# A planned attention-and-feed-forward kernel: the 42 leftover features on quarters of the array, the last block by tiles, sums shared with GpSimd, and a new plan

## The chip, the cores and the metric

The kernel runs on one core of one Trainium2 chip. The metric is the device time of one execution in microseconds (us). The core has TensorE (PE in the profile, with PEld for its weight loads), VectorE (DVE), ScalarE (ACT), GpSimd (POOL) and SyncE (SP), which here only issues transfers (DMA). Each engine works through its own instructions strictly in the order in which they were written, and waits on semaphores for the others.

## The reference, cut to what matters

The input `x` has 4 sequences of 1024 tokens with 256 features, all in 32-bit floats. After a layer norm, two branches start from the same `xn`, and both are added to `x`:

```
xn  = layernorm(x)
out = x + attention(xn) + ffn_stack(xn)

attention: rms norm, q,k,v = xn @ W_qkv (16 heads of 64), softmax over a window of 64 keys
           back, times sigmoid(xn @ W_gates + b_gates) per head, @ W_out
ffn_stack, twice (DEPTH = 2):
    h = shift_token(x)                    # second half of the features comes from the token before
    q, k, v = split(h @ wqkv)             # 8 heads of 64
    q, k = l2norm and scale, then rotary:  q*cos*s + rotate_half(q)*sin*s
    o = attention over a window of 128 keys back
    x = x + o @ wo
    h = layernorm(shift_token(x))
    a, g = split(h @ w1 + b1)             # 682 features each
    x = x + (a * gelu(g)) @ w2 + b2       # 682 = 5*128 + 42
```

The 682 hidden features are five full groups of 128 and a tail of 42 (`TAIL`).

## The kernel before, in words

The tokens are cut into 16 blocks of 256 (`TB`), each of two tiles of 128 (`NT` = 2), four blocks to a sequence. There are 16 blocks of the first attention (`first_attention(n)`), then 16 of the first feed-forward layer (`layer(0, n)`) and 16 of the second (`layer(1, n)`); the first three blocks of layer 0 (`MIX` = 3) are begun between the last blocks of the first attention. A layer's block has an attention half and, behind a `yield`, a feed-forward half. `LAG` says how many blocks' attention halves are begun before the oldest feed-forward half is recorded. What a stage leaves for the next one is stored in DRAM buffers (`carried`) and fetched again.

Nothing is written to an engine directly. Every step is recorded by `op(...)` with its cost in us on each engine that could do it, its buffers and its dependencies; `Plan.run` then goes through all steps with a model of the five engines, picks the engine where there is a choice, the time and the buffer, and `emit` writes the instructions in that order. A step is due when the steps that use it need it. The plan's constants are `SLACK` (a factor on the costs of an engine), `LAT`, `LAND` (the landing of a transfer), `LOOK` (how far ahead of the oldest open step it may reach, in us of TensorE work), the spare buffers of each kind, and the price of turning TensorE between the whole array ("full") and quarters of it ("rc", `TURN` 3.0). A transfer of n columns costs n/465 us on SP in this plan. The order that comes out is fixed; on the chip an engine that comes late makes the others wait.

The steps that the change and the prediction speak of, by their lines in the profile:

- L973 projects q, k, v of a tile ("qkvb"); L1112 are the scores ("sb") and L1202 the weighted sum over values ("ob"), both as 64x64 matmuls on quarters of the array; L1227 is the projection with `wo` ("pw").
- L1041 (GpSimd) multiplies the rotated halves with sin, L1057 (VectorE) the row with cos, L1065 (VectorE) adds the two, L1083 scales k ("kn", on either engine).
- The feed-forward half: L1235 adds the residual ("y2"), L1249, L1252 and L1257 shift half of the features by one token through transfers, L1293 to L1300 are the statistics, L1309 and the power of L401 the deviation on GpSimd, L1321 (ScalarE) or L1323 (VectorE) the normalised rows, L462 and L471 send them through DRAM and back so that L479 (VectorE) can finish a transpose, and L1336 applies gain and offset ("d"). In the last block of all, `LATE`, TensorE transposes instead (L425, L450).
- L1362 is the projection up ("up"): for each of the five full groups 2 halves x 2 chunks of 256 columns, and for the tail one matmul a chunk whose weights hold both halves of the tail side by side. L1375 (ScalarE) is the gelu, L1382 (VectorE) adds the offset and multiplies.
- L1398 is the projection down ("down"): for each tile six matmuls in a row, one for each of five groups and one for the tail, where the unused rows of the operand are zero (L1346 clears them). L1409 adds the rest, L1418 stores the output.

In 32-bit floats the profile shows every matmul as two instructions: L1398 has 64 tiles x 6 matmuls = 384, and 768 instructions.

Of the kernel before, what the change touches and what calls it, by code (L numbers as in the profile page):

```python
# [44 lines left out]
N_D = 12  # L45
LAND = 4.0
LAG = 3
MIX = 3
BOTH = True

EARLY = {0, 1}
LATE = {(1, 15)}
FROM = 8, 11

# [21 lines left out]
class Plan:  # L76
    LAT = {"PE": 0.25, "DVE": 0.3, "ACT": 0.3, "POOL": 0.3, "SP": 2.0}
    SLACK = {"DVE": 1.15, "POOL": 1.15, "ACT": 1.1}
    SWITCH = {"PE": 0.1, "ACT": 1.4}
    TURN = {"PE": 3.0, "ACT": 40.0}  # L80
    IDLE = 300.0
    LOOK = 200.0
    DEAR = {"DVE": 3.0}
# [142 lines left out]
def layers_kernel(  # L226
# [41 lines left out]
        },  # L268
        {"w": (3, 0.05, 20), "g": (1, 0.0, 1), "s": (4, 0.05, 12), "ps": (0, 0.02, 3), "d": (1, 0.0, 1)},
    )  # L270
# [15 lines left out]
    def load_x(n):  # L286
        b, g = blocks[n]
        xs[n] = xb = buf("w")
        op(
            {"SP": 1.1},  # L290
            lambda e: nc.sync.dma_start(
                v2(xb, NT, DIM), x[b, g * TB : (g + 1) * TB].rearrange("(i p) f -> p i f", p=P)
            ),
            w=(xb,), name="x",
        )
# [20 lines left out]
    def unit(pieces, us=2.3):  # L316

        u = buf("w")
        for n, (to, m, of) in enumerate(pieces):

            def bring(e, to=to, m=m, of=of):
                nc.sync.dma_start(u.t[:, to : to + m], of)

            op({"SP": max(m / 465, 0.45)}, bring, a=(u,), lat=us, name="weights")
        return u
# [50 lines left out]
    def store(dst, src):  # L376
        op(
            {"SP": 1.1},
            lambda e: nc.sync.dma_start(rows_apart(dst.t, NT * DIM), v2(src, 4, NT * DIM // 4)),
            r=(src,), w=(dst,), lat=3.5, name="store",  # L380
        )

    def fetch(src, b):
        op(
            {"SP": 1.1},
            lambda e: nc.sync.dma_start(v2(b, 4, NT * DIM // 4), rows_apart(src.t, NT * DIM)),
            r=(src,), w=(b,), name="fetch",
        )
# [40 lines left out]
    def across(s, m, turned, near=False):  # L429

        n, f = 4 * 32 * m, 32 * m
        if near:
            bank = buf("ps")
            transposes(
                lambda: [
                    (bank.t[:, k * P : (k + 1) * P], s.t[:, k * P : (k + 1) * P]) for k in range(m)  # L440
                ],
                bank, (s,), "near", 0.109 * m,
            )
            for b, to, at, k in turned:

                def put(e, b=b, to=to, at=at, k=k):
                    at = slice(at * P, (at + k) * P)
                    of = bank.t[:, at].rearrange("p (k c j) -> p j k c", k=k, j=4)
                    if e == "ACT":
                        nc.scalar.copy(to(b), of)  # L450
                    else:
                        nc.vector.tensor_copy(to(b), of)

                op(
                    {"ACT": COPY[k * P][0], "DVE": COPY[k * P][1]}, put, r=(bank,), a=(b,),
                    name="near",
                )
            return
        d = buf("d")
        op(  # L460
            {"SP": n / 465},
            lambda e: nc.sync.dma_start(rows_apart(d.t, n), v2(s, 4, f)),  # L462
            r=(s,), w=(d,), lat=LAND, name="turn out",
        )
        turn_in(d, m, turned)

    def turn_in(d, m, turned):
        n, t = 4 * 32 * m, buf("w")
        op(
            {"SP": n / 465},  # L470
            lambda e: nc.sync.dma_start(  # L471
# [16 lines left out]
    def load_layer(l):  # L488
# [31 lines left out]
        for k, (n, c) in enumerate((n, c) for n in range(2) for c in range(NC)):  # L520
# [17 lines left out]
        )  # L538
        op(
            {"SP": 0.45},  # L540
            lambda e, u=u: nc.sync.dma_start(u.t[:TAIL, DIM : 2 * DIM], w2[l, full:, :]), w=(u,),
            name="weights",
        )
        w["b1"] = bb = const.tile([P, 2, NM], F32, name=f"b1{l}")
# [21 lines left out]
    def load_rotation(l):  # L566

        for k, src in ((0, cos_d), (1, sin_d)):
# [13 lines left out]
            for q in range(2):  # L582
                u = turn[k, q] = buf("w")
                op(
                    {"SP": 1.1},
                    lambda e, u=u, q=q, src=src: nc.sync.dma_start(
# [345 lines left out]
    def layer(l, n, before):  # L932
# [29 lines left out]
        before["y"] = y  # L962
        y2 = buf("w")
        for i in range(NT):
# [67 lines left out]
            for m in range(2):  # L1032
# [20 lines left out]
                def times_cos(e, rc=rc, m=m, raw=raw, ti=ti, cos=cos):  # L1053

                    f = v3(cos, 4, 2, D)[:, ti % 4, m].rearrange("p (a r) -> p a r", a=2)
                    for h in range(2):
# [6 lines left out]
                op(  # L1063
                    {"DVE": 0.61},
                    lambda e, rc=rc, rot=rot: nc.vector.tensor_tensor(  # L1065
                        rc.t[:, :512], rc.t[:, :512], rot.t[:, :512], ALU.add
# [158 lines left out]
            def project_out(e, pw=pw, oT=oT):  # L1225
                for p in range(PB):
# [8 lines left out]
                lambda e, pw=pw, i=i: nc.vector.tensor_tensor(  # L1235
                    v3(y2, 2, NT, P)[:, :, i, :].rearrange("p c (a r) -> p c a r", a=4),
                    v3(pw, NC, 4, 32), by_feature(xb, i), ALU.add,
                ),
                r=(pw, xb), a=(y2,), name="y2",
            )  # L1240

        yield

        sh = buf("w")
        S = lambda: v2(sh, NT, P)
        y2_old = before.get("y2")

        def shift(e):
            nc.sync.dma_start(S()[0:1, 1, :], v3(y2, 2, NT, P)[P - 1 :, 1, 0, :])  # L1249

            for lo, hi in ((0, P - 16), (P - 16, P - 1)):
                nc.sync.dma_start(S()[lo + 1 : hi + 1], v3(y2, 2, NT, P)[lo:hi, 1])  # L1252

        if g:
            op(
                {"SP": 0.5},
                lambda e: nc.sync.dma_start(  # L1257
                    S()[0:1, 0, :], v3(y2_old, 2, NT, P)[P - 1 :, 1, NT - 1, :]
                ),
# [4 lines left out]
        op({"SP": 1.2}, shift, r=(y2,), a=(sh,), lat=2.4, name="sh")  # L1264
        before["y2"] = y2

# [5 lines left out]
        else:  # L1272
# [7 lines left out]
            lambda e: nc.gpsimd.tensor_tensor(  # L1280
                v3(rest, NT, 2, P), v3(y2, 2, NT, P).rearrange("p h i f -> p i h f"), to(), ALU.add
            ),
# [7 lines left out]
        def stats(e, h):  # L1290
            for i in range(NT):
                of = v3(y2, 2, NT, P)[:, 0, i, :] if h == 0 else S()[:, i, :]
                nc.vector.bn_stats(st_at(i, h), of)  # L1293
            if h:
                for i in range(NT):
                    nc.vector.bn_aggr(
                        st.t[:, 24 + 2 * i : 26 + 2 * i], st.t[:, 12 * i : 12 * i + 12]
                    )
                var = st.t[:, 24:28].rearrange("p (i s) -> p i s", i=NT)[:, :, 1]
                nc.vector.tensor_scalar_add(st.t[:, 28:30], var, EPS)  # L1300

# [4 lines left out]
        def deviation(e):  # L1306
            rsqrt(st.t[:, 30:32], st.t[:, 28:30])
            for i in range(NT):
                nc.gpsimd.tensor_scalar(shift_by(i), mean(i), rstd(i), -1.0, ALU.mult, ALU.mult)  # L1309
# [3 lines left out]
        for h in range(2):  # L1313

            def normal(e, h=h):
                for i in range(NT):
                    of = v3(y2, 2, NT, P)[:, 0, i, :] if h == 0 else S()[:, i, :]
# [10 lines left out]
        d = buf("w")  # L1328
        across(nn, 4, [(d, lambda b: b.t[:, :512].rearrange("p (k c j) -> p j k c", k=4, j=4), 0, 4)], (l, n) in LATE)

        def affine(e):
            for c in range(NC):
                at = slice(c * TB, (c + 1) * TB)
                g_, b_ = w["v"][:, 0, c : c + 1], w["v"][:, 1, c : c + 1]
# [13 lines left out]
        for m in range(NM):  # L1348
# [5 lines left out]
            def up(e, pf=pf, m=m, tail=tail):  # L1354
                for n_ in (0,) if tail else (1, 0):
                    for c in range(NC):
                        if tail:
                            wt = w["w1e"].t[:, c * P : (c + 1) * P]
                        else:
                            u, at, step = w["w1"][n_, m]  # L1360
                            wt = u.t[:, c * step + at : c * step + at + P]
                        nc.tensor.matmul(  # L1362
                            pf.t[:, n_ * TB : (n_ + 1) * TB], wt, d.t[:, c * TB : (c + 1) * TB],
                            start=(c == 0), stop=(c == NC - 1),
                        )

            op(
                {"PE": 0.86 if tail else 1.72}, up, r=(d, *us), w=(pf,),
                mode="full", name="up",
            )  # L1370

            def gelu(e, pf=pf, ge=ge, m=m, tail=tail, k=k):
                u = P // 2 if tail else 0
                at = slice(0, TB) if tail else slice(TB, 2 * TB)
                nc.scalar.activation(  # L1375
                    ge.t[:k], pf.t[u : u + k, at], AF.Gelu, bias=w["b1"][u : u + k, 1, m : m + 1]
                )

            op({"ACT": 0.39}, gelu, r=(pf, w["b_vec"]), w=(ge,), mode="gelu", name="gelu")

            def gated(e, pf=pf, ge=ge, m=m, k=k):
                nc.vector.scalar_tensor_tensor(  # L1382
                    gT[m // 2].t[:k, (m % 2) * TB : (m % 2 + 1) * TB], pf.t[:k, :TB],
                    w["b1"][:k, 0, m : m + 1], ge.t[:k], ALU.add, ALU.mult,
                )
# [5 lines left out]
        xo, xos = buf("w"), [buf("w") for _ in range(NT)]  # L1391
        for i in range(NT):
            pz = buf("ps")

            def down(e, pz=pz, i=i):
                for m in range(NM):
                    at = (m % 2) * TB + i * P
                    nc.tensor.matmul(  # L1398
                        pz.t[:, :DIM], gT[m // 2].t[:, at : at + P], v2(w["w2"][m // 2], 2, DIM)[:, m % 2, :],
                        start=(m == 0), stop=(m == NM - 1),  # L1400
                    )

            op({"PE": 2.6}, down, r=(*gT, *w["w2"]), w=(pz,), mode="full", name="down")
            xi, to_rows = xo, lambda b, i=i: by_feature(b, i)
# [135 lines left out]
```

## Time and profile before

| What | before |
|---|---|
| median of 3 runs | 1732.03 us (1731.21 to 1732.57) |
| profiled execution | 1731.92 us, of it 1730.1 us from first to last instruction |
| mean granted TensorE clock | 0.997 |
| busy: PE, DVE, ACT, POOL | 1694.0, 1322.4, 1136.5, 1143.2 us |
| moved by transfers | 357.03 MB, 206 GB/s on the average |

The profile page gives the busy time of each engine, a strip of 40 slices of the span, and groups of equal instructions with their count, busy time, mean duration and the idle time in front of them. A busy TensorE is not TensorE at its peak, since the ends of matmuls are modelled; the step from one start to the next is the safer price. Other views give the instructions in order of time, the busy time by windows, and the waits by whom they are for.

### The profile page before, as it was taken

How to read it: one execution, taken by the hardware profiler on the slowest of the kernel's cores; microseconds unless marked ns; L12 is line 12 of the kernel's file. 1: busy time of each engine (PE TensorE's matmuls, PEld its weight loads, DVE VectorE, ACT ScalarE, POOL GpSimd, SP SyncE). 2: the span in 40 equal slices, each digit the busy share in tenths (PEclk: the TensorE clock that was granted, in tenths of full speed). 3: DMA queues.
4: the chain of work that ended last, by engine and by line, in shares of the span. 5: the costliest groups of instructions: out<-in, count | busy, mean ns of one | idle time of the engine just before them, and what ended most of it. 6: DMA issues, size and time to landing. Idle time of an engine off the chain costs nothing.

```text
span 1730.1 us, 48920 instructions
## 1 busy us (share of the span) xinstructions
PE 1694.0 (98%) x16652; PEld 1294.0 (75%) x16652; DVE 1322.4 (76%) x4497; ACT 1136.5 (66%) x3428; POOL 1143.2 (66%) x1962
## 2 busy tenths in 40 slices
PE   7999999999999999899999999999999999999998
PEld 6888887888877776677777767677777777767787
DVE  4875555555556889889888899899989889988852
ACT  4766666656666876667666676767676686668652
POOL 2855345644456888868786768877877787777720
PEclk9999999999999999899999999999999999999999
DMA  7886776765756788877887777888787787776750
GB/s 213 219 244 189 202 220 174 203 195 148 197 154 201 205 234 240 243 200 226 228 234 213 222 224 204 241 228 229 216 246 222 204 234 215 211 211 195 192 152 26
DMA packets 486587, 357.03 MB, mean 206 GB/s; under 512 B 167565, under 2 KB 423745, under 8 KB 486337
## 3 DMA queue, kind: packets, MB, share of 16 engines
q1 hardware_dynamic: 485632, 353.70, 72.2%
q8 instruction: 131, 2.15, 0.5%
q14 instruction: 120, 0.98, 0.2%
q10 hardware_dynamic: 704, 0.21, 0.1%
HBM read 170.04 MB, written 146.01 MB: 183 GB/s over the span
## 4 chain that ended last, share of the span: by engine, by line
PE 53%; DVE 3%; issue 1%; ACT 1%; POOL 0%; DVEq 0%; POOLq 0%; ACTq 0%
PE ps L1362 17%; PE ps L973 14%; PE ps L1398 9%; PE ps L1227 6%; PE ps L1202 4%; PE ps L1112 3%; DVE w L479 1%; DVE w L1057 1%; ACT w L410 0%; DVE w L1133 0%; DVE s L1014 0%; ACT w L1147 0%; DVE w L1382 0%; POOL s L401 0%; POOL w L1167 0%
## 5 line engine op out<-in xcount | busy, mean ns | idle before, releaser
L410 ACT COPY w<-ps 128x256 f32<-128x256 f32 (+3 forms) x671 | 351.0, 583 | 392.1 <-PE ps L760 94.0
L479 DVE STREAM_TRANSPOSE w<-w 128x256 f32<-128x256 f32 (+2 forms) x781 | 452.2, 628 | 91.2 <-PE ps L671 44.7
L973 PE MATMUL ps<-w,w 128*128 128x512 f32 x768 | 345.0, 594 | 0.8 <-ACT w L410 0.5
L1362 PE MATMUL ps<-w,w 128*128 128x256 f32 x1408 | 314.5, 382 | 6.9 <-ACT w L1336 6.4
L849 POOL TENSOR_SCALAR w<-w,s,s 128x128 f32<-128x128 f32 x512 | 228.8, 463 | 130.3 <-DVE s L820 46.1
L1362 PEld LDWEIGHTS ps<-w,w 128*128 128x128 f32 x1408 | 268.6, 191 | 47.1 <-POOL w L1167 6.8
L1041 POOL TENSOR_TENSOR w<-w,w 128x256 f32<-128x256 f32 x256 | 205.4, 807 | 125.5 <-ACT w L410 99.0
L1167 POOL TENSOR_SCALAR w<-w,s 128x192 f32<-128x192 f32 x512 | 238.0, 483 | 56.6 <-DVE s L1159 45.2
L973 PEld LDWEIGHTS ps<-w,w 128*128 128x128 f32 x768 | 144.9, 190 | 151.7 <-issue 128.6
L401 POOL TENSOR_TENSOR s<-s,mhalf 128x16 f32<-128x16 f32 (+2 forms) x112 | 232.9, 2080 | 31.2 <-DVE s L1300 17.3
L1147 ACT ACTIVATE w<-w,s 128x192 f32<-128x192 f32 x512 | 225.9, 444 | 23.6 <-DVE w L479 5.9
L760 PE MATMUL ps<-w,w 128*128 128x256 f32 x1024 | 230.7, 383 | 1.7 <-ACT w L654 1.7
L760 PEld LDWEIGHTS ps<-w,w 128*128 128x128 f32 x1024 | 196.2, 192 | 34.8 <-ACT w L654 2.1
L830 ACT ACTIVATE w<-w,s 128x128 f32<-128x128 f32 x512 | 197.7, 391 | 12.1 <-PE ps L918 4.5
L1133 DVE CUSTOM_DVE_ANT_0 w<-ps,mask_b,s 128x192 f32<-128x192 f32 x512 | 182.2, 410 | 12.2 <-PE ps L1112 3.3
L1398 PE MATMUL ps<-w,w 128*128 128x256 f32 x768 | 171.6, 380 | 3.2 <-DVE w L1382 3.2
L1398 PEld LDWEIGHTS ps<-w,w 128*128 128x128 f32 x768 | 145.5, 190 | 33.7 <-issue 9.3
L1057 DVE TENSOR_TENSOR w<-w,w 128x256 f32<-128x256 f32 x256 | 142.5, 597 | 34.5 <-ACT w L410 25.6
L820 DVE CUSTOM_DVE_ANT_0 w<-ps,mask_a 128x128 f32<-128x128 f32 x512 | 113.3, 284 | 27.7 <-PE ps L794 20.3
L1375 ACT ACTIVATE g<-ps,b 128x256 f32<-128x256 f32 x192 | 84.5, 474 | 75.6 <-PE ps L1362 68.7
L1227 PE MATMUL ps<-w,w 128*128 128x256 f32 x512 | 126.4, 390 | 2.2 <-ACT w L410 1.5
L1202 PEld LDWEIGHTS ps<-w,w 64*64 64x64 f32 x4096 | 91.8, 133 | 41.7 <-issue 12.7
(82 smaller groups left out, 2396.4 us busy)
## 6 DMA issues: line engine op xcount, KB each, us to landing
d<-w SPq DMA_DIRECT2D x301, 256.0 KB, 3.3
w<-d SPq DMA_DIRECT2D x301, 256.0 KB, 3.4
d<-w SPq DMA_DIRECT2D x256, 192.0 KB, 3.5
w<-d SPq DMA_DIRECT2D x256, 192.0 KB, 3.2
w<-w SPq DMA_DIRECT2D x256, 128.0 KB, 3.0
w<-c SPq DMA_DIRECT2D x80, 256.0 KB, 3.5
c<-w SPq DMA_DIRECT2D x48, 256.0 KB, 3.3
w<-in_L_attn_x_dram SPq DMA_DIRECT2D x16, 256.0 KB, 5.3
```

The source lines that it names most:

```text
L401: nc.gpsimd.tensor_tensor(dst, src, mhalf.t[:, : src.shape[1]], ALU.pow)
L410: nc.scalar.copy(dst(), src())
L479: lambda e, b=b, to=to, at=at, k=k: nc.vector.transpose(to(b), v3(t, 4, m, 32)[:, :, at : at + k]),
L760: nc.tensor.matmul(pq.t[:, j * TB : (j + 1) * TB], W[c].t[:, p % GA * P : (p % GA + 1) * P], hT.t[:, c * TB : (c + 1) * TB], start=(c == 0 ...
L849: nc.gpsimd.tensor_scalar(run(s, u), run(s, u), sm.t[:, at : at + 1], gate.t[:, h : h + 1], ALU.mult, ALU.mult,)
L973: nc.tensor.matmul(p.t, y.t[:, at : at + P], w["wqkv"][m][c].t[:, :512], start=(c == 0), stop=(c == NC - 1),)
L1041: nc.gpsimd.tensor_tensor(rot.t[:, :512].rearrange("p (h u k r) -> p u k h r", h=2, u=2, k=PB)[:, u], raw[m].t[:, :512].rearrange("p (k h ...
L1147: nc.scalar.activation(v2(ex, 2, WB)[:, u].rearrange("p (a k r) -> p k a r", k=3, a=2), v2(s, 2, WB)[:, u].rearrange("p (k a r) -> p k a r ...
L1167: nc.gpsimd.tensor_scalar(v2(ex, 2, WB)[:, u], v2(ex, 2, WB)[:, u], sm.t[:, at : at + 1], 1.0, ALU.mult, ALU.mult,)
L1227: nc.tensor.matmul(pw.t[:, :DIM], v3(oT, 2, 2, P)[:, p % 2, p // 2], v2(w["wo"][p // 2], 2, DIM)[:, p % 2, :], start=(p == 0), stop=(p == ...
L1362: nc.tensor.matmul(pf.t[:, n_ * TB : (n_ + 1) * TB], wt, d.t[:, c * TB : (c + 1) * TB], start=(c == 0), stop=(c == NC - 1),)
L1398: nc.tensor.matmul(pz.t[:, :DIM], gT[m // 2].t[:, at : at + P], v2(w["w2"][m // 2], 2, DIM)[:, m % 2, :], start=(m == 0), stop=(m == NM - 1),)
```

## The change

- **Tail.** The 42 rows of `w2` are loaded twice, at partitions 0 and 64. The product of gate and offset is written per tile (two instructions, tile 0 to partitions 0 to 41, tile 1 to 64 to 105). "down" keeps the five full groups (10 instructions a tile instead of 12); a new step `down_last` ("last", mode "rc") adds the tail for both tiles with four 64x64 matmuls of 256 columns, one on each quarter of the array.
- **Last block.** For (1, 15) (`APART`) the second half runs per tile (`after_attention` with `ts` of one tile): own shift, statistics, transposes, "up" on 128 columns, gelu and product. Its "last" is done per tile, on two quarters.
- **Sums.** The sum of rotated rows may run on GpSimd (cost 1.35) as well as on VectorE (0.61).
- **Plan.** `RATE` 540 in place of 465 for all transfers, `LAND` 3.7 for 4.0, `LAG` 2 for 3, `BOTH` off (some copies, the normalising and the gain only on ScalarE), `SLACK` 1.05, 1.05 and 1.15 for 1.15, 1.15 and 1.1 (DVE, POOL, ACT), `LOOK` 120 for 200, more spare buffers of kind "w", and the weights of layer 1 asked for at block 13 of layer 0 instead of 11. The order comes out anew on all engines.

```diff
-LAND = 4.0
-LAG = 3
+RATE = 540.0
+LAND = 3.7
+LAG = 2
-BOTH = True
+BOTH = False
+APART = {(1, 15)}
-FROM = 8, 11
+FROM = 8, 13
...
-    SLACK = {"DVE": 1.15, "POOL": 1.15, "ACT": 1.1}
+    SLACK = {"DVE": 1.05, "POOL": 1.05, "ACT": 1.15}
-    LOOK = 200.0
+    LOOK = 120.0
...
-        {"w": (3, 0.05, 20), ...
+        {"w": (4, 0.1, 30), ...
...
-            {"SP": n / 465},
+            {"SP": n / RATE},
...
+        for k in range(2):
+            def last_rows(e, u=u, at=k * P // 2):
+                nc.sync.dma_start(u.t[at : at + TAIL, DIM : 2 * DIM], w2[l, full:, :])
...
-                    {"DVE": 0.61},
-                    lambda e, rc=rc, rot=rot: nc.vector.tensor_tensor(
+                    {"DVE": 0.61, "POOL": 1.35},
+                    lambda e, rc=rc, rot=rot: {"DVE": nc.vector, "POOL": nc.gpsimd}[e].tensor_tensor(
...
+        for ts in [[i] for i in range(NT)] if apart else [list(range(NT))]:
+            y2_old, before["y2"] = before.get("y2"), y2s[ts[-1]]
+            after_attention(l, n, w, y2s[ts[0]], y2_old, ts)
...
+                if tail:
+                    for i in ts:
+                        at, to = slice(i * P, (i + 1) * P), i * P // 2
+                        nc.vector.scalar_tensor_tensor(
+                            gT[-1].t[to : to + k, TB + i * P : TB + (i + 1) * P], pf.t[:k, at],
+                            w["b1"][:k, 0, m : m + 1], ge.t[:k, at], ALU.add, ALU.mult,
+                        )
+                    return
...
-                for m in range(NM):
+                for m in range(NM - 1):
                     at = (m % 2) * TB + i * P
                     nc.tensor.matmul(
                         pz.t[:, :DIM], gT[m // 2].t[:, at : at + P], v2(w["w2"][m // 2], 2, DIM)[:, m % 2, :],
-                        start=(m == 0), stop=(m == NM - 1),
+                        start=(m == 0), stop=False,
                     )
...
+        def down_last(e):
+            h = P // 2
+            for i, pz in pzs.items():
+                for k in range(2):
+                    r, at = slice(i * h, (i + 1) * h), TB + i * P + k * h
+                    nc.tensor.matmul(
+                        pz.t[k * h : (k + 1) * h, :DIM], gT[-1].t[r, at : at + h],
+                        w["w2"][-1].t[r, DIM : 2 * DIM], start=False, stop=True,
+                    )
+        op({"PE": 0.45}, down_last, r=(gT[-1], w["w2"][-1]), a=(*pzs.values(),), mode="rc", name="last")
```

In the order that the new plan writes, 77 of the 128 sums stand on GpSimd and 51 on VectorE; of the 64 scalings of k, 28 stand on GpSimd (before 44). TensorE turns between whole array and quarters 92 times one way and 91 back (before 93 and 93).

## The prediction

> **What bounds the kernel now.** I read the page's busy times first, then the windows around the one dip of the clock, then TensorE in order of time, and last the engines that feed it.
>
> ```profile
> span 1730.1 us, 48920 instructions
> PE 1694.0 (98%) x16652; PEld 1294.0 (75%) x16652; DVE 1322.4 (76%) x4497; ACT 1136.5 (66%) x3428; POOL 1143.2 (66%) x1962
> L1398 PE MATMUL ps<-w,w 128*128 128x256 f32 x768 | 171.6, 380 | 3.2 <-DVE w L1382 3.2
> L1057 DVE TENSOR_TENSOR w<-w,w 128x256 f32<-128x256 f32 x256 | 142.5, 597 | 34.5 <-ACT w L410 25.6
> L1041 POOL TENSOR_TENSOR w<-w,w 128x256 f32<-128x256 f32 x256 | 205.4, 807 | 125.5 <-ACT w L410 99.0
> ```
>
> TensorE is busy for 98% of the span, so its own work sets the time; what can go beside it is some 36 us of idle time. The last two rows are the products that compete on VectorE and GpSimd.
>
> ```profile
> 600.00:700.00 100.00, 100.00 (x1139) 72.07 (x1132) 91.57 (x302) 72.94 (x230) 89.13 (x143) 1.00 0.81 232
> 1200.00:1300.00 100.00, 100.00 (x803) 72.76 (x802) 92.34 (x260) 70.41 (x188) 77.03 (x118) 1.00 0.80 229
> 720.90:727.60 6.70, 0.42 (x2) 0.02 (x1) 6.70 (x23) 3.84 (x17) 6.53 (x9) 0.69 0.75 224
> 727.60:733.70 6.10, 5.99 (x14) 4.85 (x15) 3.48 (x8) 3.07 (x6) 3.84 (x9) 0.50 0.96 267
> ```
>
> Columns: window, length, then busy us of PE, PEld, DVE, ACT, POOL, the clock, the transfers' share and GB/s. In the feed-forward stage PE is full, DVE near 90 and POOL near 77; where the first attention ends (600 to 700) both are near 90. Right after that comes the one large hole: TensorE idles, and then runs 6.1 us at half clock.
>
> ```profile
> 719.33 1.99 PE L1227 MATMUL ps<-w,w 128*128 128x256 f32 x8
> 727.71 12.70 PE L1362 MATMUL ps<-w,w 128*128 128x256 f32 x44 [6.39 <-ACT w L1336]
> ...
> 1160.24 5.34 PE L1398 MATMUL ps<-w,w 128*128 128x256 f32 x24
> 1165.52 1.57 PE L1202 MATMUL ps<-w,w 64*64 64x128 f32 x64
> 1166.90 1.48 PE L1112 MATMUL ps<-w,w 64*64 64x192 f32 x32
> 1168.32 1.99 PE L1227 MATMUL ps<-w,w 128*128 128x256 f32 x8
> 1170.15 3.60 PE L973 MATMUL ps<-w,w 128*128 128x512 f32 x8
> ...
> 1683.17 1.03 PE L1362 MATMUL ps<-w,w 128*128 128x256 f32 x4
> 1685.27 5.45 PE L1398 MATMUL ps<-w,w 128*128 128x256 f32 x24 [1.07 <-DVE w L1382]
> ```
>
> Prices come from starts. L1398: 24 instructions in 1165.52 - 1160.24 = 5.28 us, 0.10 of it the turn to quarters, so 0.216 each. L1112: 32 quarter matmuls of 192 columns in 1.42 us; as eight waves of four at once that is 8 x 192 = 1536 columns, 0.92 ns a column. L1202 gives the same: 32 of 128 and 32 of 64 columns are 1536 in waves, in 1.38 us. L1227 takes 1.83 before L973, against 8 x 0.216 = 1.73: 0.10 for turning back.
>
> **The change part by part.** Sums are against the profiled execution, 1731.92 us (span 1730.1 and 1.8 around it); the median of the runs is 0.1 above.
>
> Tail on quarters. Removed in each of 31 blocks: 2 tiles x 2 instructions x 0.216 = 0.864 us. Added: 8 quarter instructions of 256 columns, two waves x 256 x 0.92 ns = 0.47 us; I take 0.46. That is -0.40 a block, **-12.5 us**. In the last block two waves of two remain for each tile: 0.92 against 0.864, nothing. Bounds: -13.4 if a wave costs the full array's 0.216, and +26.8 if the eight ran one after the other (8 x 0.216 = 1.73 against 0.864, x 31), which L1112 and L1202 contradict.
>
> Turns. In the new order 30 of the 33 "last" stand beside another quarter step, 27 of them between L1202 and L1112, and turns fall from 93 + 93 to 92 + 91: nothing. The Trainium skill's "TensorEngine Tiling (Array Packing)", Key Properties, speaks against this part: it says that changing the tiling mode drains TensorE. The trace agrees, with about 0.10 us each way; were each "last" alone, that would be 33 x 0.20 = 6.6 us given back.
>
> The hole at 720.9. The idle time is 6.4 us; the first 44 "up" take 12.63 us to the next start against 44 x 0.216 = 9.50, so half clock costs 3.1: 9.5 together. L1336 came late because the chain behind it (shift, statistics, transposes on DVE, deviation on POOL) ran through the stretch where both are at 90; from the end of L1227 it took 84 us in this block, and the order gave it 75 us of TensorE work as cover. Of the sums in the first three blocks of layer 0, 8 of 12 go to GpSimd: 8 x 0.735 = 5.9 us leave DVE there. The hole was 6.4. I take it as gone: **-9.5** (bounds 0 and -9.5). Late next would be the "up" of the following blocks, below.
>
> Ends. "down" waits behind the tail's product three times (blocks 13 to 15 of layer 1), 1.24 us a time over the step of 0.216. The new order puts quarters, transposes or two "last" between, 0.4 to 1.4 us: **-2** (0 to -3.7). L1227 idles 2.2 us after L1202; "last" adds 0.46 of cover in 27 places: **-1** (0 to -2.2).
>
> The shorter lag. This adds waits. From the end of the second "pw" of a block to the end of L1336 the trace has 34.0 to 36.6 us in the quickest blocks of steady work, and 29.0 where work thins out (pw ends 1661.7, L1336 ends 1690.7). With its own rows alone (y2 0.42, shift 2.4, statistics 1.0, deviation 1.3, normalising 1.7, out and in 0.5 + 3.3 and 0.5 + 3.4, transpose 1.1, gain 1.1) it needs 17. Counting TensorE's work between the two in each order, cover falls from 65 to 77 us to 33.6 to 35.4 in 22 blocks, and less in (0,2) 25.3, (0,3) 31.9, (0,4) 30.2, (0,5) 27.0, (0,7) 30.2, (1,13) 26.7, (1,14) 20.5. With 29.0 needed, the blocks below it lack 3.7 + 2.0 + 2.3 + 8.5 = 16.5 us; with 17, none. The chain's long values had time to spare, so it can be quicker than 29; queues on SP and DVE keep it from 17. I take the middle, **+8** (0 to 16.5), and none in the 22 blocks. Behind a late L1336 wait all 11 "up" matmuls, L1375 and L1382; the next block's L973 stands behind them on TensorE.
>
> Sums on GpSimd. 77 x 1.273 (the POOL row for 128x512, L1280) = 98 us more there, 77 x 0.735 = 57 less on DVE. For k, 16 scalings go back: POOL -16 x 2 x 0.636 = 20, DVE +16. The tail's product is two instructions: DVE +31 x (0.2 to 0.46), 6 to 14. So DVE falls by some 30 us and POOL rises by 78, over the 1130 us of these stages 90 to 87% and 77 to 84%. Neither becomes the bound: 0 on the path, if the order holds. Cover gone, a GpSimd step late by one sum delays L479 behind it by 1.3 us.
>
> The Trainium skill's "GPSIMD Engine Reference", Specifications, says that GpSimd shares its SBUF interfaces with VectorE and collides with VectorE instructions of two SBUF inputs. The trace agrees: L1057 runs 377 ns at best and 597 on the mean, L1041 719 and 807. By it (597 - 426, the median) x 256 = 44 us are lost on DVE for 205 us of L1041, so 98 us more could cost 21 there, still less than the 30 it gains.
>
> Last block by tiles. 88 "up" instructions of 128 columns for 44 of 256: at the transposes' step of 0.11 the same 9.5 us, at the weight load's 0.191 mean 16.8. The four transposes of L425 (0.60 with their four loads) are the nearer row: 0 (up to +7). More instructions on DVE, ACT, POOL and five more transfers on SP lie beside TensorE.
>
> Transfers. 540 columns a us are 540 x 512 B = 276 GB/s; the window at 727.6 moved 267 at a share of 0.96, 278 at full. The plan is then only truer; bytes hardly change: 0. The later weights of layer 1 (block 13) have three blocks of 34 us: 0.
>
> Sum: 1731.9 - 12.5 - 9.5 - 2 - 1 + 8 = 1714.9, the median **1715**.
>
> **The rivals.**
> All waits go: the new order has no lack and the ends close: -13.4 - 9.5 - 3.7 - 2.2 gives 1703. For it speaks that steady blocks now have nearly no wait; against it (1,14), with 20.5 us of cover.
>
> Slower, by the shorter lag in each block: if the chain stays at the 36.6 us of block (1,13) under more POOL work, each of 22 blocks waits about 2 us more than its cover of 34.4, 48 us, and 1731.9 - 25 + 8 + 48 gives 1763. It decides from 0.8 us a block on (17/22). For it: 34.0 us is the quickest steady chain seen. Against it: those chains stood idle in queues that the old order had no reason to shorten.
>
> The hole only moves: a late "up" in (0,2) to (0,5) idles as long and halves the clock as well, without the gain of 9.5: 1724.
>
> Each "last" pays its own turns: 1715 + 6.6 = 1722. Not done at once on four quarters: 1715 + 12.5 + 26.8 = 1754.
>
> **How the numbers follow.** The runs spread over 0.08%; about 0.2% (3.5 us) is what a measurement of this kernel can tell from no change. Chances: 1715 as summed 0.55, all waits gone 0.18, hole moved 0.12, own turns 0.03, a wait in each block 0.10, serial quarters 0.02. The first four are faster unless new waits reach the upper end together (16.5, the weight loads' 7 and the hole kept: 1731.9 - 15.5 + 23.5 = 1740), for which I take 0.02 off: faster 0.86, same 0.04, slower 0.10. The range leaves out the slower cases and the lowest tip: 1702 to 1730.
>
> **What would show it.** "last" as 256 quarter instructions of 256 columns, steps of waves near 0.23; 640 for "down"; no half clock in mid-span; PE's span of work 12 us shorter. Wrong would be: "up" waiting for L1336's successor by 1 us or more in most blocks, a second dip of the clock, or "last" at 0.8 us.

## The result and the profile after

The changed kernel takes **1720.34 us** (median of 4 runs, 1718.14 to 1722.05), the kernel before 1731.62 beside it (1730.20 to 1732.57). The ratio is **0.9936, with a 95% interval of 0.9924 to 0.9949**: 11.3 us faster. The forecast was 1715 in 1702 to 1730, that is 17 us faster; the number lies in the range, 5.3 us off the point. The profiled execution took 1720.48 us, 11.4 less than the one before.

The head of the page of the changed kernel, the sum of its stages from 735 to 1660 us (total, then busy us of each engine), and its groups of equal instructions (line, engine, operation, shapes, count | busy us, mean ns | idle time before them):

```profile
span 1718.7 us, 49347 instructions
PE 1679.1 (98%) x16824; PEld 1278.8 (74%) x16824; DVE 1308.0 (76%) x4487; ACT 1143.4 (67%) x3442; POOL 1207.9 (70%) x2010
...
sum 925.00, PE 916.79 PEld 665.96 DVE 800.81 ACT 648.23 POOL 752.53; mean PE 458.40 PEld 332.98 DVE 400.41 ACT 324.11 POOL 376.26
...
L1449 PE MATMUL ps<-w,w 128*128 128x256 f32 x640 | 144.8, 380 | 2.4 <-DVE w L1428 1.1 <-ACT w L1366 0.9 <-DVE s L1139 0.3
L1463 PE MATMUL ps<-w,w 64*64 64x256 f32 x256 | 20.2, 378 | 0.0
L1063 DVE TENSOR_TENSOR w<-w,w 128x256 f32<-128x256 f32 x256 | 139.4, 590 | 48.7 <-ACT w L412 39.5 <-PE ps L1208 3.7 <-PE ps L887 3.4
L1071 POOL TENSOR_TENSOR w<-w,w 128x512 f32<-128x512 f32 x77 | 98.9, 1292 | 5.5 <-DVE w L1063 3.3 <-POOL w L1047 0.8
```

The same sum before was PE 921.22, DVE 816.97, ACT 629.09, POOL 690.61. TensorE still fills the span. The lines have moved: "down" (L1398) is L1449 and has 640 instructions, "last" is L1463 with 256; L973, L1112, L1202, L1227 and L1362 are now L979, L1118, L1208, L1233 and L1403; L1041, L1057 and L1065 are L1047, L1063 and L1071; L1336, L1382 and L1409 are L1377, L1433 (the tail's L1428) and L1475. Other lines that appear below: L412 copies results of TensorE on ScalarE (before L410) and L481 transposes on VectorE (before L479); L1020 sums squares and L1139 adds the mask to the scores, both on VectorE; L1153 takes the exponentials on ScalarE; L1484 stores a tile of the output. The buffers `ps` are the banks of PSUM, the memory that TensorE writes its products to.

The changed kernel in order of time (start, length, line, shapes, count, idle time before it and what ended that): TensorE in the stretch that held the hole, a steady block with VectorE's lines beside it, and the end.

```profile
714.15 2.32 PE L1449 MATMUL ps<-w,w 128*128 128x256 f32 x10
716.31 10.46 PE L979 MATMUL ps<-w,w 128*128 128x512 f32 x24
726.70 1.53 PE L1118 MATMUL ps<-w,w 64*64 64x192 f32 x32
728.05 0.61 PE L1463 MATMUL ps<-w,w 64*64 64x256 f32 x8
...
1273.28 0.61 PE L1463 MATMUL ps<-w,w 64*64 64x256 f32 x8
1273.72 1.48 PE L1118 MATMUL ps<-w,w 64*64 64x192 f32 x32
1276.04 1.97 PE L1233 MATMUL ps<-w,w 128*128 128x256 f32 x8 [0.84 <-DVE w L1475]
...
1272.82 1.81 DVE L1063 TENSOR_TENSOR w<-w,w 128x256 f32<-128x256 f32 x2
1274.55 0.68 DVE L1071 TENSOR_TENSOR w<-w,w 128x512 f32<-128x512 f32 x1
1275.16 0.74 DVE L1475 TENSOR_TENSOR w<-ps,w 128x256 f32<-128x256 f32 x2
...
1682.66 9.82 PE L1403 MATMUL ps<-w,w 128*128 128x256 f32 x44 [1.05 <-ACT w L1377]
...
1698.24 7.75 PE L1403 MATMUL ps<-w,w 128*128 128x128 f32 x68
1705.83 2.32 PE L1449 MATMUL ps<-w,w 128*128 128x256 f32 x10
```

There is no hole near 720 us and the clock is whole. "last" takes 1273.72 - 1273.28 = 0.44 us for both tiles. But L1233 behind the scores now waits for L1475, which empties the PSUM banks that "last" completes. "last" ends at 1273.28 + 0.61 = 1273.89; VectorE is then still at two products (L1063) and a sum (L1071) of rotated rows, and begins L1475 only at 1275.16. The 68 products of 128 columns take 7.59 us, 0.112 each.

To see where the rest went, I matched each step of TensorE's order with its instructions in the trace, took start to next start, and subtracted the price of an undisturbed step (0.216 for each full-array instruction of 256 columns, 0.432 for "last", and so on). What is left is turns and waits, called surplus here. All kernels of this study:

| kernel | ratio to before (95%) | VectorE busy | work | surplus 0-540 | 540-735 | 735-1660 | end |
|---|---|---|---|---|---|---|---|
| before | 1 | 1322.4 | 1636.3 | 31.8 | 17.9 | 27.4 | 5.3 |
| changed | 0.9936 (0.9924-0.9949) | 1308.0 | 1623.1 | 34.1 | 8.0 | 36.8 | 5.8 |
| tail_full | 1.0018 (1.0009-1.0028) | 1305.8 | 1636.4 | 36.9 | 8.3 | 37.0 | 5.9 |
| tail_only | 0.9979 (0.9970-0.9989) | 1326.2 | 1622.4 | 27.3 | 17.5 | 37.3 | 7.4 |
| code_only | 0.9950 (0.9935-0.9964) | 1315.6 | 1623.1 | 28.6 | 12.5 | 41.0 | 3.3 |
| const_only | 1.0057 (1.0038-1.0075) | 1336.0 | 1636.3 | 30.0 | 11.4 | 39.1 | 5.8 |
| sums_dve | 1.0026 (1.0015-1.0036) | 1338.0 | 1623.1 | 33.0 | 8.7 | 49.7 | 6.0 |
| no_share | 1.0017 (1.0006-1.0028) | 1336.8 | 1623.1 | 33.6 | 9.6 | 39.6 | 12.4 |
| both_on | 1.0022 (1.0013-1.0032) | 1337.7 | 1623.1 | 33.8 | 12.1 | 42.7 | 6.2 |
| lag3 | 0.9956 (0.9941-0.9971) | 1308.7 | 1623.1 | 33.3 | 10.8 | 37.8 | 5.3 |
| land375 | 0.9960 (0.9945-0.9975) | 1307.0 | 1623.1 | 34.2 | 11.6 | 34.9 | 5.4 |
| no_apart | 0.9946 (0.9931-0.9961) | 1304.9 | 1622.4 | 36.6 | 7.5 | 37.8 | 5.6 |
| dve_light | 0.9918 (0.9899-0.9938) | 1282.3 | 1623.1 | 32.8 | 7.6 | 31.8 | 6.1 |
| act_light | 0.9920 (0.9903-0.9937) | 1306.9 | 1623.1 | 33.0 | 7.2 | 37.0 | 6.0 |

The profiled execution was the fastest of its kernel for code_only, const_only, sums_dve, both_on, land375 and dve_light, and the slowest for tail_full, no_apart and act_light, so their surplus is low or high by some us. The first two rows give the account: work -13.2, surplus +2.3 in the first attention, **-9.9** from 540 to 735, **+9.4** from 735 to 1660, +0.5 at the end. Comparisons with the changed kernel go over the ratios to before, and 0.001 is 1.7 us; each column of one profiled execution carries some us of scatter between runs.

### The profile page after: what moved, and what is told of

It is laid out like the page before. It is cut to its first block, busy times and chain, and to the rows that moved or that the text cites. A ratio compares the mean times of both kernels' runs of the same rounds, so it can differ in the third digit from the quotient of the medians.

```text
span 1718.7 us, 49347 instructions
## 1 busy us (share of the span) xinstructions
PE 1679.1 (98%) x16824; PEld 1278.8 (74%) x16824; DVE 1308.0 (76%) x4487; ACT 1143.4 (67%) x3442; POOL 1207.9 (70%) x2010
## 5 line engine op out<-in xcount | busy, mean ns | idle before, releaser
L412 ACT COPY w<-ps 128x512 f32<-128x512 f32 (+2 forms) x661 | 340.7, 582 | 326.1 <-PE ps L764 96.7
L481 DVE STREAM_TRANSPOSE w<-w 128x256 f32<-128x256 f32 (+2 forms) x781 | 455.8, 628 | 104.1 <-DMA w<-d 57.0
L979 PE MATMUL ps<-w,w 128*128 128x512 f32 x768 | 347.2, 595 | 1.4 <-DVE s L1139 0.9
L1403 PE MATMUL ps<-w,w 128*128 128x256 f32 (+1 forms) x1452 | 313.6, 374 | 2.1 <-ACT w L1377 1.1
L1403 PEld LDWEIGHTS ps<-w,w 128*128 128x128 f32 x1452 | 267.7, 190 | 49.5 <-issue 5.2
L403 POOL TENSOR_TENSOR s<-s,mhalf 128x16 f32<-128x16 f32 (+3 forms) x113 | 230.5, 2040 | 77.1 <-DVE s L624 52.2
L1153 ACT ACTIVATE w<-w,s 128x192 f32<-128x192 f32 x512 | 226.4, 444 | 44.8 <-DVE s L1139 11.2
L979 PEld LDWEIGHTS ps<-w,w 128*128 128x128 f32 x768 | 144.1, 190 | 149.5 <-issue 128.6
L1047 POOL TENSOR_TENSOR w<-w,w 128x256 f32<-128x256 f32 x256 | 198.9, 782 | 66.0 <-ACT w L412 48.0
L764 PE MATMUL ps<-w,w 128*128 128x256 f32 x1024 | 229.5, 382 | 1.7 <-DMA w<-in_L_attn_W_qkv_dram 1.7
L764 PEld LDWEIGHTS ps<-w,w 128*128 128x128 f32 x1024 | 195.7, 192 | 34.7 <-issue 2.2
L834 ACT ACTIVATE w<-w,s 128x128 f32<-128x128 f32 x512 | 198.2, 389 | 30.3 <-issue 11.6
L1139 DVE CUSTOM_DVE_ANT_0 w<-ps,mask_b,s 128x192 f32<-128x192 f32 x512 | 181.5, 409 | 9.0 <-PE ps L1118 5.5
L1063 DVE TENSOR_TENSOR w<-w,w 128x256 f32<-128x256 f32 x256 | 139.4, 590 | 48.7 <-ACT w L412 39.5
L1417 ACT ACTIVATE g<-ps,b 128x256 f32<-128x256 f32 (+1 forms) x198 | 87.1, 467 | 93.1 <-PE ps L1403 83.6
L1449 PE MATMUL ps<-w,w 128*128 128x256 f32 x640 | 144.8, 380 | 2.4 <-DVE w L1428 1.1
L1449 PEld LDWEIGHTS ps<-w,w 128*128 128x128 f32 x640 | 120.8, 190 | 30.6 <-issue 7.6
L1233 PE MATMUL ps<-w,w 128*128 128x256 f32 x512 | 125.7, 388 | 3.8 <-DVE w L1475 3.0
L1208 PEld LDWEIGHTS ps<-w,w 64*64 64x64 f32 x4096 | 92.0, 133 | 37.3 <-issue 24.5
```

Of the source, the lines that this page charges most:

```text
L403: nc.gpsimd.tensor_tensor(dst, src, mhalf.t[:, : src.shape[1]], ALU.pow)
L412: nc.scalar.copy(dst(), src())
L481: lambda e, b=b, to=to, at=at, k=k: nc.vector.transpose(to(b), v3(t, 4, m, 32)[:, :, at : at + k]),
L764: nc.tensor.matmul(pq.t[:, j * TB : (j + 1) * TB], W[c].t[:, p % GA * P : (p % GA + 1) * P], hT.t[:, c * TB : (c + 1) * TB], start=(c == 0 ...
L834: nc.scalar.activation(of(ex, u), v2(s, GA, P)[:, u].rearrange("p (k a r) -> p k a r", k=2, a=2), AF.Exp, bias=sm.t[:, at : at + 1], scale ...
L979: nc.tensor.matmul(p.t, y.t[:, at : at + P], w["wqkv"][m][c].t[:, :512], start=(c == 0), stop=(c == NC - 1),)
```

## The experiments

Five keep the changed kernel's order and alter one thing in it (tail_full, sums_dve, dve_light, act_light, and, up to the last block, no_apart); in the others the order was planned anew.

**1. The tail on the whole array (tail_full).**

```diff
-                for k in range(2):
-                    r, at = slice(i * h, (i + 1) * h), TB + i * P + k * h
-                    nc.tensor.matmul(pz.t[k * h : (k + 1) * h, :DIM], gT[-1].t[r, at : at + h], ...)
+                at = TB + i * P
+                nc.tensor.matmul(pz.t[:, :DIM], gT[-1].t[:, at : at + P], ...)
```

> The changed kernel with every instruction in its place, but the step 'last' does the tail with one matmul on the whole array for each tile (two in place of four quarter matmuls; the other rows of its operands are zero). Theory A (the tail's work on TensorE is the gain, and the planned order gives part of everything else back in small waits): a block takes 0.864 us in place of 0.43 to 0.47 for the tail, and 27 of these steps now stand between two quarter steps and pay up to 0.2 us of turns: 13 us slower from the work, up to 5 from the turns, so 1733 to 1739. Theory B (the gain is the new plan, the tail's work hides in waits): within 4 us of 1720.

It took 1734.69 us; 1.0018 against 0.9936 is 14.2 us, and the trace has 13.3 us more work. Theory A is right: the quarters are worth what the two waves of four made one expect, and the surplus behind 540 us stays where it was (8.3, 37.0 and 5.9 against 8.0, 36.8 and 5.8).

**2. The sums back on VectorE, order kept (sums_dve).**

```diff
-  lambda e, rc=rc, rot=rot: {"DVE": nc.vector, "POOL": nc.gpsimd}[e].tensor_tensor(
+  lambda e, rc=rc, rot=rot: nc.vector.tensor_tensor(
```

> The changed kernel with every instruction in its place, but the 77 sums that the plan put on GpSimd are issued on VectorE at the same point of the order. Theory A: VectorE gets 77 x 0.7 = 54 us back and GpSimd loses 98, VectorE goes from some 88% to 92% in the feed-forward stage, and the copies and transposes behind it come late: 3 to 20 us slower, 1723 to 1740. Theory C (the sums on GpSimd are what makes the new small waits, by contention and by queueing behind them): 3 to 8 us faster, 1712 to 1717.

It took 1735.08 us, 15.6 us more than the changed kernel by the ratios. The same work stands on TensorE; the surplus from 735 to 1660 us goes from 36.8 to 49.7. Windows of this kernel (total, busy PE, PEld, DVE, ACT, POOL, clock, transfers' share, GB/s), its VectorE rows for the two products, and the step that shows it best:

```profile
735.00:1200.00 465.00, 456.15 (x3988) 327.93 (x3988) 415.51 (x1189) 323.81 (x854) 344.69 (x520) 1.00 0.78 221
1200.00:1660.00 460.00, 452.79 (x4059) 326.73 (x4058) 405.85 (x1160) 314.65 (x834) 329.53 (x508) 1.00 0.75 215
...
L1063 DVE TENSOR_TENSOR w<-w,w 128x256 f32<-128x256 f32 x256 | 133.3, 565 | 42.5 <-ACT w L412 34.8 <-PE ps L1208 2.8 <-PE ps L887 2.0
L1071 DVE TENSOR_TENSOR w<-w,w 128x512 f32<-128x512 f32 x128 | 92.5, 727 | 2.0 <-POOL w L1047 0.9
...
1324.53 1.57 PE L1208 MATMUL ps<-w,w 64*64 64x128 f32 x64
1328.01 2.12 PE L1118 MATMUL ps<-w,w 64*64 64x192 f32 x32 [1.91 <-ACT w L412]
1330.06 3.04 PE L979 MATMUL ps<-w,w 128*128 128x512 f32 x4
1332.93 1.89 PE L1233 MATMUL ps<-w,w 128*128 128x256 f32 x8
```

VectorE is busy for 821.4 of 925 us (89%) instead of 800.8 (87%), and that is enough to add 13 us of waits in small pieces. The largest of that stretch is the one shown: 1.91 us for L1118 (1.36 in the changed kernel), and then half clock, so that four L979 take 2.87 us from start to start, against four times 0.43. Theory C, that the sums on GpSimd bring the waits, is wrong; they take waits away.

**3. The code alone, with the former plan's constants (code_only), and 4. the constants alone (const_only).**

```diff
 code_only: changed kernel with
-LAND = 3.7, LAG = 2, BOTH = False, FROM = 8, 13, RATE = 540.0, SLACK 1.05/1.05/1.15, LOOK = 120.0, "w": (4, 0.1, 30)
+LAND = 4.0, LAG = 3, BOTH = True,  FROM = 8, 11, RATE = 465.0, SLACK 1.15/1.15/1.1,  LOOK = 200.0, "w": (3, 0.05, 20)
 const_only: kernel before with the first of these lines
```

> The code of the change (tail on quarters, last block by tiles, sums shared) with all constants of the plan as before (465, 4.0, lag 3, both engines for the copies, the old slacks, look 200). Theory A: -13 us of TensorE work as in the changed kernel; more turns (207 in place of 186) cost 2; the hole behind the first attention may stay (9.5) or go: 1709 to 1722. Theory B: near the kernel before, 1727 to 1733.

> The kernel before with only the new constants of the plan. Theory A: the tail's 13 us stay, the hole goes (-9.5), and small waits of 8 to 12 us come in its place: 1728 to 1735. Theory B: the plan is the gain: 1718 to 1724.

code_only took 1722.15 us, at the upper edge of its Theory A: 9.5 faster than before by the medians, 2.4 us behind the changed kernel by the ratios, with overlapping intervals. At the place of the hole "up" still waits, though shorter, and TensorE's clock stays whole behind it:

```profile
718.16 5.51 PE L1403 MATMUL ps<-w,w 128*128 128x256 f32 x24 [2.57 <-ACT w L1377]
```

const_only took 1740.54, 8.9 us slower than before, beyond what either theory gave. The constants make the former code slower: in that code all 128 sums are on VectorE, and the new order has 39.1 us of surplus from 735 to 1660 where the former had 27.4. It has no hole near 720 us (11.4 from 540 to 735).

**5. BOTH on again (both_on), 6. the lag back at 3 (lag3), 7. another landing time (land375), 8. the last block whole (no_apart).**

```diff
 both_on:  -BOTH = False          +BOTH = True
 lag3:     -LAG = 2               +LAG = 3
 land375:  -LAND = 3.7            +LAND = 3.75
 no_apart: -APART = {(1, 15)}     +APART = set()
```

> The changed kernel with the normalisations allowed on VectorE again (BOTH back to True); the order is planned anew, 66 sums go to GpSimd where the changed kernel sent 77. Theory A (the waits that came new between 1200 and 1660 us are those of ScalarE's copies behind other work, at L1118, L979 and L1233, and part of them goes when ScalarE has less to do): the excess of that stage falls from 17.3 to some 13 us and the time is 1714 to 1718 us. Rival L (the new waits are what any other order of equal work leaves somewhere, not ScalarE's): 1718 to 1727 us, with the waits in other places and no smaller sum. Rival S (the shorter lag is what makes them): within 1 us of the changed kernel, 1719 to 1721.5 us.

> The changed kernel with the lag back at 3, planned anew; all else stays. Theory S (the prediction's: the shorter lag brings waits of some 8 us, though they were not found in the products named): the time falls to 1711 to 1716 us. Theory A (nothing hangs on the lag, ScalarE's copies and held PSUM buffers do): 1718 to 1722 us. Rival L (any new order moves the time by some us to either side): 1717 to 1727 us, with the waits of other pairs.

> The changed kernel with one planned time of transfers at 3.75 instead of 3.7 us: a change with no meaning of its own, which still gives another order (82 sums on GpSimd for 77). It measures what an order is worth by itself. Rival L (orders of equal work differ by some us): away from the changed kernel by 2 to 7 us, to 1714 to 1718 or 1722 to 1728 us. Theories A and S (the waits have causes that stay the same here): 1718.5 to 1722 us.

> The changed kernel with the last block's feed-forward of both tiles at once again (APART empty); up to there the order is the same. The prediction has the last block by tiles at 0, between a gain of some us and a loss of 7. Theory P (its products at 128 columns cost as much as at 256 in all, and the chain of one tile hides that of the other): without it the end waits for the shift, the normalisation and the transposes of both tiles, 1722 to 1727 us. Rival Q (the end was covered by the products of earlier blocks anyway): 1719 to 1721.5 us. Rival R (more instructions and single waits cost more than they hide): 1714 to 1718 us.

both_on took 1734.31 us, and all three theories missed it by 7 us or more. The planner used the freedom to put 42 copies and 4 normalisations more on VectorE and to take 11 sums back to it: VectorE's busy time rises by 29.7 us, and the time by 14.9 us by the ratios, nearly as in sums_dve. ScalarE has 19.6 us less, which buys nothing.

lag3 took 1723.77 us. Theory S is wrong: the longer lag gains nothing, so the prediction's +8 us for the shorter one has no ground. land375 took 1724.08 us; lag3 and it lie 3.5 and 4.2 us behind the changed kernel by the ratios, with intervals that overlap a little. That is what an order of the same work and the same VectorE time can be worth, and it bounds what may be read into any single replanned run. no_apart took 1721.98 us, 1.7 behind with overlapping intervals: the last block by tiles costs nothing and gains too little to be told.

**9. VectorE lighter (dve_light), 10. ScalarE lighter (act_light).** Both in the changed kernel's order.

```diff
 dve_light, L1021: -v2(sq, HB, D), AX.X, ALU.add
                   +v2(sq, HB, D)[:, :, : D // 2], AX.X, ALU.add
 act_light, L1014: -sq.t[:, :512], raw[m].t[:, :512], AF.Square
                   +sq.t[:, :256], raw[m].t[:, :256], AF.Square   (and L1021 reads the 256 columns twice)
```

> The changed kernel in its own order; the 128 sums of squares at L1020 read 32 of each head's 64 elements, so that part of the norm is left out and VectorE has some 35 us less to do (128 times about half of 666 ns). Theory V (what came back as new waits after 735 us is VectorE's queue: PSUM buffers held until L1475, L1433 and L1139 have run): the excess of 735 to 1660 us falls from 36.8 to 30 us or less, and the time is 1712 to 1716 us. Theory A (it is ScalarE's copies at L412) and Rival L (it is the order, and no single engine): 1718.5 to 1722 us.

> The changed kernel in its own order; the 128 squares at L1013 are taken of 256 columns instead of 512, and the sums behind them read these twice, so that half of the heads' norms are left out, ScalarE has some 35 us less to do (128 times about half of 636 ns) and VectorE as much as before. Theory A (the new waits are for ScalarE's copies at L412, which stand behind other work): the excess of 735 to 1660 us falls from 36.8 to 30 us or less, and the time is 1712 to 1716 us. Theory V (VectorE's queue) and Rival L (no single engine): 1718.5 to 1722 us.

The two lines are L1020 and L1013 in the profile. VectorE lost 25.7 us of work in the one, ScalarE 25.3 us in the other. The times are 1717.04 and 1717.76 us, both between the ranges of the two theories. By the ratios they are 3.1 and 2.8 us faster than the changed kernel, with intervals that overlap its own, and they can't be told apart; as times the pair is inconclusive. It does bound what is left: these 25.7 us off VectorE are worth some 3 us, well below 14. In the traces the surplus from 735 to 1660 falls to 31.8 in dve_light and stays at 37.0 in act_light, with the reserve made above for both. The place of the largest wait is plainer. Changed kernel, in order of time, lines of PE, VectorE, SyncE's queue and ScalarE:

```profile
1308.65 1.48 PE L1118 MATMUL ps<-w,w 64*64 64x192 f32 x32
1310.90 1.97 PE L1233 MATMUL ps<-w,w 128*128 128x256 f32 x8 [0.77 <-DVE w L1475]
1320.88 1.53 PE L1118 MATMUL ps<-w,w 64*64 64x192 f32 x32 [1.36 <-ACT w L412]
...
1308.53 0.65 DVE L1071 TENSOR_TENSOR w<-w,w 128x512 f32<-128x512 f32 x1
1309.10 1.02 DVE L481 STREAM_TRANSPOSE w<-w 128x384 f32<-128x384 f32 x2
1310.05 0.71 DVE L1475 TENSOR_TENSOR w<-ps,w 128x256 f32<-128x256 f32 x2
...
1310.45 0.83 SPq L1484 DMA_DIRECT2D out_dram<-w  x2
...
1314.47 1.28 ACT L1153 ACT_TABLE_LOAD   x1 [2.69 <-DMA out_dram<-w]
1319.76 1.56 ACT L412 COPY w<-ps 128x512 f32<-128x512 f32 x3 [0.37 <-PE ps L1208]
```

and dve_light, the same steps:

```profile
1304.31 1.48 PE L1118 MATMUL ps<-w,w 64*64 64x192 f32 x32
1305.72 1.99 PE L1233 MATMUL ps<-w,w 128*128 128x256 f32 x8
1314.18 1.48 PE L1118 MATMUL ps<-w,w 64*64 64x192 f32 x32
...
1304.63 0.72 DVE L1475 TENSOR_TENSOR w<-ps,w 128x256 f32<-128x256 f32 x2
...
1305.05 0.83 SPq L1484 DMA_DIRECT2D out_dram<-w  x2
...
1307.35 1.28 ACT L1153 ACT_TABLE_LOAD   x1 [0.96 <-DMA out_dram<-w]
```

Read it from the first L1118 on. In the changed kernel VectorE is behind: L1475 begins 1.40 us after L1118's start, the stores of its result 1.80 after, and ScalarE's exponentials, whose buffer is by the trace the one being stored, begin 5.82 after, having stood idle for 2.69 us. The copies behind them come late, and L1118 waits 1.36 us for ScalarE's L412. In dve_light the same steps come 0.32, 0.74 and 3.04 us after, and both waits of TensorE are gone. In act_light the wait is even longer, though ScalarE has less to do:

```profile
1318.94 1.53 PE L1118 MATMUL ps<-w,w 64*64 64x192 f32 x32 [1.92 <-ACT w L412]
```

The trace names ScalarE, but the cause at this place is VectorE's queue, with a buffer and a transfer between. The 1.36 and the 0.77 are together 2.1 us, of 9.4 that came back.

**11. No sharing, planned for it (no_share), 12. the tail alone (tail_only).**

```diff
 no_share:  changed kernel     -{"DVE": 0.61, "POOL": 1.35}   +{"DVE": 0.61}
 tail_only: code_only          -{"DVE": 0.61, "POOL": 1.35}   +{"DVE": 0.61}
                               -APART = {(1, 15)}             +APART = set()
```

> The changed kernel with all 128 sums of rotated rows on VectorE, and the order planned for that (before, 77 of them were moved back in an order that was planned for the sharing, and it took 14.7 us). Theory A (sharing gives room that any order can use): 1726 to 1735 us. Rival L (it was the order that did not fit; planned for it, the sums cost what another order costs): 1719 to 1726 us.

> The kernel before with the tail's product on quarters and nothing else: its planned costs and due times, all sums on VectorE, the last block whole; the order is planned anew. Theory P (the prediction's: 12.5 us of work go, and the hole at 720.9 us goes with any new order): 1712 to 1720 us. Theory A (the order before was a good one between 735 and 1660 us, where every other order so far has 7 to 15 us more excess, which takes back what the hole gives): 1717 to 1724 us. Rival C (it needs the sharing to come out): 1725 us or more.

no_share took 1733.05 us, 14.0 us more than the changed kernel by the ratios and slower than before (1.0006 to 1.0028). So the loss in sums_dve was not only that of an order that didn't fit: Theory A is right about the time. But it is not lost in the same place. Of the 11.0 us between the two profiled executions, 2.8 lie in the surplus from 735 to 1660 us (12.9 in sums_dve) and 6.6 behind 1660, most of it at one wait, of block (1,13):

```profile
1667.91 11.38 PE L1403 MATMUL ps<-w,w 128*128 128x256 f32 x44 [3.70 <-ACT w L1377]
```

"up" waits 3.70 us for its gain there, and 3.4 us of half clock, worth 1.7, begin with it; in the changed kernel the same 44 instructions start without a wait.

tail_only took 1726.77, 3.6 us faster than before by the ratio, where its 13.9 us less work should have given more. It kept the hole, as TensorE in order of time and the window behind it show:

```profile
713.56 1.99 PE L1233 MATMUL ps<-w,w 128*128 128x256 f32 x8
722.25 12.79 PE L1403 MATMUL ps<-w,w 128*128 128x256 f32 x44 [6.69 <-ACT w L1377]
...
720.00:728.00 8.00, 5.75 (x14) 4.60 (x15) 6.46 (x11) 3.66 (x6) 6.22 (x13) 0.50 0.90 266
```

tail_only has 37.3 us of surplus from 735 to 1660, 9.9 more than before. Theory P is wrong: not any new order closes the hole. Rival C is right in the number: under the old constants and without the sharing, the tail gives only 3.6 us.

## Why the prediction was right or wrong

**Tail on quarters, -12.5: right.** 13.2 us of work are gone, and undoing it costs 14.2. "last" measures 0.44 us beside another quarter step, where 0.46 was taken. **Turns, 0:** nothing in the runs speaks against it.

**The hole, -9.5: right in size (-9.9), not shown in cause.** The prediction took it as gone because VectorE had 5.9 us less to do there. Under the old constants the wait falls from 6.69 us (tail_only) to 2.57 (code_only), which differ by the sharing and by the last block; so the sharing may shorten it, but doesn't close it. Under the new constants it is gone in const_only and in no_share too, with every sum on VectorE. So the new constants close it without the sharing; which of them does that is open.

**Ends, -2, and cover of L1227, -1: wrong.** The surplus at the end rose by 0.5; L1449 still waits 1.13 us for the tail's gate, and L1403 waits 1.05. L1233 waits 3.0 us in five places for L1475 where L1227 had waited 2.2 in all. The cover came, but the prediction had not seen that both tiles' banks can be emptied only after "last", by instructions that stand behind other work in VectorE's queue.

**The shorter lag, +8: too large, and in the wrong blocks.** "up" waits once for L1377, 1.05 us in block (1,14), the block with the least cover. Of the two bounds for the chain, 29 and 17 us, the lower was the nearer. lag3, where no "up" waits for L1377, is no faster. That 9.4 us of new surplus did come after 735 us is no support for this step; it is in other steps. The margin is thin, though: with the same lag and all sums on VectorE (no_share) one "up" waits 3.70 us.

**Sums on GpSimd, 0 on the path: the step that failed.** Row by row the forecast of the load was good: from before to the changed kernel the sums left 52 us less on VectorE (92.4 to 40.3; 57 forecast), the scalings brought 13 more (16) and the tail's product 10 more (6 to 14). As a whole VectorE's busy time fell by 14.4 us only, from 88% to 87% of the time from 735 to 1660 us, and GpSimd's rose from 75% to 81%. What failed is the inference behind it: "neither becomes the bound: 0 on the path". Undoing the sharing costs 15.6 us in the same order and 14.0 in one of its own.

**What was not in the sum: the former order was a good one.** Its 27.4 us of surplus from 735 to 1660 is the lowest of all fourteen kernels. The same code under the new constants has 39.1, the tail alone under the old ones 37.3. Every new order that was run has lost that; no term stood for it. No run gave the former order the lighter tail, so what that order was worth is read from the surplus and not from a time. Sharing the sums is what the new plan needed to come out ahead: without it, it is slower than before by 3 us in spite of 13 us less work.

So two errors offset each other: a part priced at 0 that is worth some 14 us, and a loss through the new order priced at 8 us, in the wrong place, that is larger. Taking the measured 11.3 faster, less the tail's 14.2 and the sharing's 14.0, all the rest together costs some 17 us, hole included, where the prediction had it gain 4.5 (parts undone one at a time need not add up exactly). That the point came within 5.3 us is luck, and the number held because the range was drawn from the rivals and not from this sum. No rival described what happened.

## What to carry to other kernels

An engine that is busy for 87 to 90% of a stage is not the bound, but its queue can be what the bound waits for: here the kernels with 29 to 30 us more on VectorE took 14 to 16 us more, in sums_dve, no_share and both_on. The price is not a fixed rate: code_only, with 7.6 us more on VectorE than the changed kernel, is not clearly slower, and 25.7 us less in dve_light gained some 3. Price a shift of work between such engines by the waits that it feeds, not by asking which engine becomes the bound. And where a planner writes the order, a change of its inputs throws away the order that was there: look at how little the old one waits, and charge the loss.

The name beside a wait is the last link of a chain. Follow it back until something stood idle for want of work or something was queued; here, at the place looked at, a wait "for ScalarE" was VectorE's delay, passed on by a store.

## What the runs showed of the hardware

**Half clock can follow a short wait.** Over all fourteen traces, the windows of 4.5 us behind the idle times of TensorE above 1 us, its first wait and the two holes aside, show a clock of 0.62 to 0.66 behind 1.65 us (no_share), 1.91 (sums_dve), 1.92 (tail_full), 2.39 (const_only), 2.86 (code_only) and 3.70 (no_share), and a whole one behind all others, among them 1.65 and 1.92 (act_light), 1.93 (lag3), 2.2 (changed) and 2.57 (code_only). So the length alone doesn't decide: the same L1118 waits 1.91 us in sums_dve and 1.92 in act_light. Where it fell, it was half for 3.4 us, and for 10.2 at the holes of 6.39 (before) and 6.69 us (tail_only). One short stretch, from sums_dve:

```profile
1328.80:1332.20 3.40, 3.40 (x23) 1.72 (x16) 3.40 (x12) 3.40 (x10) 3.19 (x5) 0.50 0.83 194
1332.20:1335.00 2.80, 2.80 (x12) 2.09 (x12) 2.80 (x11) 2.80 (x14) 0.08 (x1) 1.00 0.79 247
```

The Trainium skill's "TensorE: Matmul & The Clock Gate", HAM oscillation, gives as a rule that there should be no idle gaps above about 3.4 us; these runs show half clock behind gaps of half that length, and not behind all of them, so the measurement decides here. The 3.4 us for which it lasts agrees with the window that the page gives in Part 1.

**Two engines at one memory.** In the same order, with 77 sums of 1292 ns more on GpSimd, L1063 on VectorE takes 590 ns instead of 565, and the 51 sums left there 794 instead of the 739 that the same 51 take in sums_dve: 6.4 and 2.8 us. GpSimd's own L1047 stays at 782 (789). The Trainium skill's "GPSIMD Engine Reference", Specifications, says that such instructions collide; the runs agree, and the loss on these two lines stays below the 21 us that the prediction had worked out as its upper end.
